# Seven small reorderings in a four-layer kernel whose order is written out by hand: weights and norms, MLP rows, image loads of a spectral layer, products of an attention, and idle matmuls

## The chip, the cores and the metric

The kernel runs on one core of one Trainium2 chip, in fp32. The time is what the device takes for one execution, in microseconds (us). TensorE is called PE, VectorE DVE, ScalarE ACT, GpSimd POOL; SP is the queue that issues most of the transfers (DMA). PE and its weight load (PEld) are shown apart.

## The reference, cut to what matters

The input x has the shape (4, 56, 56, 128): batch, rows, columns, channels. Four layers are added to it in turn, each after a group norm `_gn` over 32 groups.

```python
x = x + L0(_gn(x))      # windows 7x7 shifted by 3, 4 heads; then global attention; then an MLP
x = x + L1(_gn(x))      # edge layer
x = x + L2(_gn(x))      # spectral attention and two spectral MLP layers
x = x + L3(_gn(x))      # convolution over rows, sums over rows and columns

# L0, the second half, on xf = (B, 3136, 128)
xf = xf + _mha(_layernorm(xf, g1, be1), ...)
h = gelu(_layernorm(xf, g2, be2) @ w1 + b1)         # 128 -> 512
xf = xf + (h @ w2 + b2)                             # 512 -> 128

# L1
edge = relu(proj_i[:, :, :, None, :] + proj_j[:, :, None, :, :] + be)
node = relu(concat([x, edge.sum(axis=3)]) @ Wn.T + bn)

# L2: each of the (batch, row) images is 56 columns x 128 channels, normed; 32 heads
k, q, v = spectral convolutions of the normed image   # rfft2, 16x16 modes kept at both ends, irfft2
attn = softmax(q k^T / sqrt(d))                       # over the 56 rows
projd = spectral convolution of attn @ v
attention = inorm(projd + x)
m = gelu(inorm(spec(inorm(attention))) + skip); m = inorm(spec(m)) + skip
out = inorm(m) + attention

# L3
y = conv(x, W, kernel 3 over rows) + b
out = relu((y.sum(columns) + y.sum(rows) - y) / sqrt(H + W - 2) + x)
```

## The kernel before, in words

The function `build` runs the stages one after the other. Every engine executes its instructions in the order in which the program writes them, so that the Python order of the calls, and of `next(...)` on generators that emit a few instructions each, is the schedule. Transfers on SP are issued in order too: a request that waits for an engine holds those behind it.

*Input norms* (`input_norms`, 0 to 50 us). The four images of 128 x 3136 are loaded and normed as they land (`norm_steps`), and the lengths of the largest query and key vectors are bounded (`products`, `longest`). The generator `weights` puts pieces between: `score_bounds`, `attention_bias` (b_p, L906 to L923) and `edge_weights`. `fill(n)` emits n idle matmuls `z_p<-c_ones` of 128x384, each in two passes, to keep PE at work. The last one is `fill(4)`, ahead of the first real matmul, L375.

*Four batches* (50 to 2587 us). Each runs `fast_windows` (the shifted windows), `fast_layer` (global attention and MLP) and `edge_layer`. The attention works on seven query blocks of 448; `values(room)` issues the products with the values as chunks get ready, and `remainder(j)` one odd chunk of block j. The MLP takes eight row groups: `hidden(wi)` makes four matmul pairs into banks (L779) and GELUs on ACT (L780), `result(wi)` four more into the bank `pm[:, 4]` (L800), which DVE adds to the row (L802) and POOL (for the last one DVE) adds to the image (L813, L815). L770 is DVE's norm of a row group, which the `hidden` of that group reads.

*Spectra* (`spectra`, 2587 to 2668 us). For each of the four images `first_transform` does the transform along the columns in four pieces of 14 rows (`s_pr<-t_images,s_x`, L1655), and `sample_spectra` the rest (L1671, L1683, L1693). The images 0 to 2 come from the scratch `xad` in two halves each, in two buffers `s_x2`; image 3 is still in the tile `x1`. `normed_images` norms image 3 in steps (`go_on(n)` takes n of them): statistics, then four pieces of 128x784 normed on DVE by `apply_norm`, and its transfer to `xat`. `all_score_weights` and `value_weights` compute the weights of the attention, mostly on POOL (L1750 to L1796); their inputs come by SP.

*Attention weights* (`attention_weights`, 2668 to 2801 us). For two pairs of images (bp) and sixteen channels c, the spectrum times the weights `q_g` is built as `q_u`, one half on DVE (L1864, n = 0) and one on POOL (L1862, n = 1), and PE multiplies it with the spectrum into `q_acc` (L1877, 16 matmuls each). The list `seq` gives the order; `make` runs four items ahead of `product`. After sixteen channels `collect` copies `q_acc` to y, and `softmax` turns y (L1911, L1919) into weights; `skips` prepares the skip terms.

*Attend* (`attend`, 2801 to 3123 us). DVE (`u_ud`, L2018) and POOL (`u_up`, L2020) build scaled images, and PE mixes them with the weights `AT` into `u_po` (L2023).

*Outputs* (`outputs`, 3123 to 3463 us). Projection, norms, spectral MLP and the convolution (L2683) of all batches are operations of a class `Plan`, issued in an order that is written out as a list of numbers (`OUTPUT_ORDER`). PE's small matmuls on `o_sq` (L2339) and `o_r` (L2366) make sums and norms there; L2272 and L2255 are transforms.

Of the kernel before, what the change touches and what calls it, by code (L numbers as in the profile page):

```python
# [19 lines left out]
P = 128  # L20
# [603 lines left out]
def fast_layer(k, w, xw, xf, x1, st, beside, mr, shift):  # L624
# [9 lines left out]
    with ExitStack() as es:  # L634
# [158 lines left out]
        def result(wi):  # L793
            ts, hT = parts[wi], made.pop(wi)
            po = pm[:, 4, :N]
# [21 lines left out]
        with tc.manual_schedule(engines={mybir.EngineType.PE, mybir.EngineType.Activation, mybir.EngineType.DVE}):  # L817
# [31 lines left out]
            while t < 96 * NBLK:  # L849
                scores(0)  # L850
                scores(1)
                values(ROOM[turn % 4] + (len(ready) > 3))
# [3 lines left out]
                if special < NBLK and t >= 96 * special + 7 and (not special or hasattr(blocks[special - 1], "raw")):  # L856
                    j = special
                    special += 1
                    remainder(j)
# [32 lines left out]
            for wi in range(3, 8):  # L892
                if wi < 7:
                    hidden(wi + 1)
                result(wi)
# [65 lines left out]
def input_norms(k, x, pool, wk, psum, weights):  # L961
# [49 lines left out]
    fill(2)  # L1011
    next(steps[3])
    next(steps[3])
    products(2)
    longest(2)
    next(work)
    next(work)
    products(3)
    next(work)
# [6 lines left out]
    for _ in range(2):  # L1026
        next(work)
# [524 lines left out]
def normed_images(k, w, st, b, wk, bank, xp, xad, xat):  # L1552
# [49 lines left out]
    nc.vector.tensor_scalar_mul(mean, mean, mr[:, 1:2])  # L1602
    yield
# [16 lines left out]
    def normed():  # L1620
        for t in range(0, HH, 14):
            apply_norm(k, x[:, t:t + 14, :], x[:, t:t + 14, :], mr)
            if t < 42:
                yield
# [17 lines left out]
def first_transform(k, st, b, pools, x, to):  # L1642
# [7 lines left out]
    xf = x.rearrange("p t h -> p (t h)")  # L1650
# [48 lines left out]
def spectra(k, w, st, xat, images):  # L1699
# [7 lines left out]
    with ExitStack() as es:  # L1707
# [7 lines left out]
        first = [first_transform(k, st, b, (wk, psum), st.x1 if b == B - 1 else images(b), zs) for b in range(B)]  # L1715
# [10 lines left out]
        fill(3)  # L1726
        go_on(28)
        next(first[0])
        next(first[0])
        go_on(1)  # L1730
        fill(4)
        next(first[0])
        go_on(1)
        next(first[0])
        go_on(2)
        for b in range(B):
            for n, _ in enumerate(sample_spectra(k, st, b, (wk, psum), zs.pop(b))):
                go_on(2)
# [72 lines left out]
def attention_weights(k, I, w, st):  # L1811
# [9 lines left out]
    with ExitStack() as es:  # L1821
# [21 lines left out]
        for bp in range(2):  # L1843
            for c in range(16):
                seq += [(bp, c, 0, None), (bp, c, 1, None)]
                if c in (8, 10, 12, 14):
                    seq.insert(len(seq) - 1, (bp, None, c // 2 % 2, c // 12))

# [76 lines left out]
        ahead = 4  # L1925
        for item in seq[:ahead]:
            make(*item)
        for n, item in enumerate(seq):
# [12 lines left out]
            if n >= 3 and between and next(between[0], 0) == 0:  # L1941
# [7 lines left out]
def attend(k, I, w, st, dd, xat, xm, softmax, beside, psum):  # L1949
# [4 lines left out]
    with ExitStack() as es:  # L1954
# [50 lines left out]
        late = []  # L2005
        prepare(0)
        for turn, (g, n, bp) in enumerate(turns):
# [5 lines left out]
            for i in range(2):  # L2013
                for h0, m, e in (shares if turn else first)[left < 16]:
# [6 lines left out]
                    for q in range(m):  # L2021
# [4 lines left out]
                        left -= 1  # L2026
                    for step in steps.get((turn, left), ()):
# [149 lines left out]

class Plan:
# [4 lines left out]
    def __init__(self, **buffers):  # L2183
        self.ops, self.buffers = [], buffers
# [8 lines left out]
    def issue(self, order):  # L2193
# [7 lines left out]
        for n in order:  # L2201
            op = self.ops[n]
            assert all(a.end for a in op.after)
            for b, key in op.takes:
                taken[b].append(key)
                old = len(taken[b]) - 1 - self.buffers[b]
                assert old < 0 or not users[b, taken[b][old]]
            op.run()
            op.end = True
            for g in op.gives:  # L2210
                users[g] -= 1

# [556 lines left out]
def outputs(k, w, st, ys, x2d, xm, out, psum):  # L2769

    tc = k.tc
    with ExitStack() as es:
# [3 lines left out]

        def bank():
            return psum.tile([P, 512], F32, tag="b", name="o_b")

        def banks():  # L2780
            taken[0] += 1
            tag, bufs = ("x", 1) if taken[0] % 3 == 0 else ("px", 2)
            return psum.tile([P, 2, 512], F32, tag=tag, name="o_d", bufs=bufs)
# [20 lines left out]
        for b, op in ((1, wholes[3].spread[0]), (2, wholes[3].factors)):  # L2804
            for p in wholes[b].convolve:
                p.after.append(op)
        plan.issue([int(n) for n in OUTPUT_ORDER.split()])
# [29 lines left out]
def build(k, packs, I, out):  # L2837
# [3 lines left out]
    with ExitStack() as es:  # L2841
# [9 lines left out]
        x1 = x1w[:, :HH, :]  # L2851
        dd = dp.tile([3, 4, 2, 16, NB], F32, name="dd")
# [5 lines left out]
        with tc.tile_pool(name="w01", bufs=1) as wp, tc.tile_pool(name="io", bufs=1) as io:  # L2858
            xw = io.tile([P, TOK], F32, name="xw")
            with ExitStack() as pre:  # L2860
# [18 lines left out]
                def weights(ps):  # L2879
                    yield from score_bounds(k, w0, bounds, wk, ps)  # L2880
                    added = attention_bias(k, w0, wp)
                    edge_weights(k, w1, wp)
                    yield
                    added()
                    yield
# [4 lines left out]
                small_scores = scores_are_small(k, bounds, wp, wk)  # L2890

            def first_layers(front, x, to, loaded=False):
# [4 lines left out]
                front(k, w0, xw, xf, x1, st)  # L2897
                edge_layer(k, w1, x1, st)
# [14 lines left out]
            with small.Else():  # L2913
# [4 lines left out]
                with tc.tile_pool(name="n_x", bufs=2) as xs, tc.tile_pool(name="n_ps", bufs=2, space=PSUM) as psum:  # L2918
                    for b in range(B - 1):
                        xp = xs.tile([P, HH, HH], F32, name="n_x")  # L2920
                        nc.sync.dma_start(xp, x2d[b])
                        for _ in normed_images(k, w2, st, b, io, lambda: psum.tile([P, 512], F32, name="n_ps"), xp,
                                               xad, xat):
                            pass

        x2s = ExitStack()
        x2p = x2s.enter_context(tc.tile_pool(name="x2", bufs=2, side="right"))

        def images(b):
            if b not in loaded:  # L2930
                xp = loaded[b] = x2p.tile([P, HH + 1, HH], F32, name="s_x2")
                for o in (slice(0, 29), slice(29, HH)):
                    nc.sync.dma_start(xp[:, o, :], xad[b, :, o, :])
                nc.gpsimd.memset(xp[:, HH, :], 0.0)
            return loaded[b]

        loaded = {}
        for b in range(2):
            images(b)
        nc.sync.dma_start(x2d[B - 1], x1)  # L2940
# [52 lines left out]
```

## Time and profile before

| | us |
|---|---|
| median of three runs | 3463.82 (3462.63 to 3465.51) |
| the profiled execution | 3464.84 |
| its span in the profile | 3463.1 |

The profile's span is from the first to the last instruction of the profiled execution; that execution's own time is 1.0 us over the median. Its granted clock, the TensorE clock that the throttle allowed, has a mean of 0.993 of full speed.

| stage | window, us | length | PE busy |
|---|---|---|---|
| input norms | 0 to 50.14 | 50.14 | 29.27 |
| four batches | 50.14 to 2587.2 | 2537.06 | 2459.28 |
| spectra | 2587.2 to 2668 | 80.80 | 76.49 |
| attention weights | 2668 to 2801.4 | 133.40 | 123.08 |
| attend | 2801.4 to 3122.7 | 321.30 | 316.39 |
| outputs | 3122.7 to 3463.1 | 340.40 | 314.51 |

A row of a wait names the engine, the tile and the line that waited, and behind the arrow the engine and line that came last. A row of the timeline has the start, the length, the operation with its output and inputs, the count of passes, and in brackets the idle time before it and its releaser. A matmul of fp32 takes two passes in these counts, so that one idle matmul is x2.

### The profile page before, as it was taken

What the parts mean: (1) busy time and instruction counts of PE and PEld (TensorE: products, weight loads), DVE (VectorE), ACT (ScalarE), POOL (GpSimd) and SP (SyncE); (2) the same over time, 40 slices, a digit from 0 to 9 for tenths busy, and PEclk for the clock granted to TensorE, in tenths of its full rate; (3) what the DMA queues carried; (4) which work ended last, traced back from release to release, by engine and by line L of the source; (5) the groups of instructions that cost most, each with busy time, mean ns of one, the idle gap of its engine ahead of it and who ended that gap; (6) DMA issues with size and microseconds to landing.
All of it is one profiled execution on the core that took longest, in us unless ns stands there. A gap on an engine that the chain in (4) does not pass through costs nothing. (4 is left out here: it accounts for less than half of the span.)

```text
span 3463.1 us, 64456 instructions
## 1 busy us (share of the span) xinstructions
PE 3319.0 (96%) x27800; PEld 1425.6 (41%) x27800; DVE 2657.9 (77%) x2555; ACT 2131.1 (62%) x2253; POOL 1285.9 (37%) x796
## 2 busy tenths in 40 slices
PE   7999999999999999999999999999999999999998
PEld 4433333353333435333343443333337433336664
DVE  6588867867888696788859858887794778895776
ACT  4688876668888575788857668887653012215442
POOL 1000007800000491000019400000775778884786
PEclk9999999999999999999999999999999999999999
DMA  2143420024434000444310033442014037743101
GB/s 106 43 94 89 97 54 19 20 53 93 92 91 86 19 1 20 106 103 91 91 42 1 20 81 90 93 97 54 1 40 118 1 87 187 190 115 94 57 20 56
DMA packets 98012, 243.41 MB, mean 70 GB/s; under 512 B 64457, under 2 KB 69833, under 8 KB 92713
## 3 DMA queue, kind: packets, MB, share of 16 engines
q0 software_dynamic: 16128, 102.77, 14.8%
q1 hardware_dynamic: 74872, 123.61, 12.2%
q10 hardware_dynamic: 6720, 12.85, 1.3%
q8 instruction: 220, 3.60, 0.4%
q14 instruction: 72, 0.58, 0.1%
HBM read 79.43 MB, written 31.33 MB: 32 GB/s over the span
## 5 line engine op out<-in xcount | busy, mean ns | idle before, releaser
L830 ACT ACTIVATE f_ring<-f_pm 128x1792 f32<-128x1792 f32 (+1 forms) x764 | 1093.8, 1482 | 226.4 <-PE f_pm L827 179.6
L682 DVE TENSOR_TENSOR f_acc<-f_acc,f_ring 128x1792 f32<-128x1792 f32 x468 | 947.5, 2025 | 190.2 <-ACT f_ring L830 160.0
L827 PE MATMUL f_pm<-f_qT,f_kT 32*128 32x448 f32 x5376 | 722.6, 571 | 9.9 <-ACT f_p L716 4.1
L672 POOL DMA_DIRECT2D f_far<-f_ring x112 | 96.5, 862 | 1328.2 <-ACT f_ring L830 1033.4
L693 PE MATMUL f_pm<-f_ring,f_va 128*32 128x448 f32 (+1 forms) x6304 | 589.4, 490 | 0.0
L1269 POOL TENSOR_TENSOR e_tp<-e_a,e_c 128x1792 f32<-128x1792 f32 (+2 forms) x172 | 480.4, 2831 | 36.7 <-issue 36.7
L1267 DVE TENSOR_TENSOR e_td<-e_a,e_pc 128x1792 f32<-128x1792 f32 (+2 forms) x292 | 478.3, 1703 | 8.8 <-ACT e_c L1255 8.8
L827 PEld LDWEIGHTS f_pm<-f_qT,f_kT 32*128 32x128 f32 x5376 | 260.2, 183 | 411.5 <-ACT f_ring L830 300.3
L693 PEld LDWEIGHTS f_pm<-f_ring,f_va 128*32 128x32 f32 x6304 | 163.8, 109 | 410.1 <-issue 397.8
L1271 ACT ACTIVATE e_tp<-e_tp 128x1792 f32<-128x1792 f32 (+2 forms) x172 | 253.3, 1495 | 98.0 <-POOL e_tp L1269 98.0
L2018 DVE TENSOR_TENSOR u_ud<-u_px,u_d 112x1792 f32<-112x1792 f32 x144 | 263.4, 1863 | 39.7 <-PE u_po L2023 35.1
L2020 POOL TENSOR_TENSOR u_up<-xh,u_d 112x1792 f32<-112x1792 f32 (+1 forms) x72 | 240.9, 3373 | 55.0 <-PE u_po L2023 40.7
L1338 PE MATMUL e_acc<-e_td,t_edge 128*32 128x448 f32 x1952 | 231.6, 542 | 6.6 <-DVE e_td L1267 6.4
L2023 PE MATMUL u_po<-u_ud,AT 112*64 112x448 f32 x1056 | 213.9, 544 | 1.9 <-DVE u_ud L2018 1.9
L1338 PE MATMUL e_acc<-e_tp,t_edge 128*32 128x448 f32 x1184 | 147.9, 543 | 23.7 <-ACT e_tp L1271 23.7
L2023 PEld LDWEIGHTS u_po<-u_ud,AT 112*64 112x64 f32 x1056 | 74.3, 138 | 128.9 <-issue 112.8
L1338 PEld LDWEIGHTS e_acc<-e_td,t_edge 128*32 128x32 f32 x1952 | 61.6, 110 | 142.6 <-issue 93.7
L737 DVE RECIPROCAL f_den<-f_den 128x448 f32<-128x448 f32 x28 | 82.6, 2951 | 44.9 <-ACT f_den L734 44.9
L1862 POOL TENSOR_TENSOR q_u<-iS,q_g 128x1792 f32<-128x1792 f32 x32 | 102.8, 3235 | 22.8 <-PE q_acc L1877 22.8
L813 POOL TENSOR_TENSOR x<-xf,xw 128x343 f32<-128x343 f32 x28 | 25.5, 911 | 224.7 <-DVE xf L802 224.7
L1877 PE MATMUL q_acc<-q_u,S 64*64 64x448 f32 x1024 | 104.4, 552 | 4.4 <-DVE q_u L1864 3.3
L2121 ACT COPY x_ev<-x_po 56x896 f32<-56x896 f32 x32 | 28.8, 900 | 126.9 <-DMA x_xs<-xat 51.1
(525 smaller groups left out, 4579.1 us busy)
## 6 DMA issues: line engine op xcount, KB each, us to landing
f_far<-f_ring POOLq DMA_DIRECT2D x112, 896.0 KB, 6.4
u_d<-dd SPq DMA_DIRECT2D x46, 784.0 KB
f_far<-f_ring SPq DMA_DIRECT2D x28, 896.0 KB
xw<-in_x SPq DMA_DIRECT2D x4, 1568.0 KB
x2d<-x SPq DMA_DIRECT2D x4, 1568.0 KB
xat<-x SPq DMA_DIRECT2D x4, 1568.0 KB
x_xs<-xat ACTq DMA_DIRECT2D x32, 196.0 KB
xm<-x_ev ACTq DMA_DIRECT2D x64, 98.0 KB
```

The costliest lines, as they stand in the source:

```text
L682: nc.vector.tensor_add(e.acc, e.acc, slots(j, c))
L693: nc.tensor.matmul(e.po[heads[h], part], va[o, c, heads[h]], p, start=(c == 0), stop=(c == 23 and part.stop == NB))
L827: nc.tensor.matmul(ss[:, i, :NB], kT[heads[h], c * P:(c + 1) * P], qT[heads[h], blk(j)], start=True, stop=True)
L830: nc.scalar.activation(ring[:, slot:slot + m, :], ss[:, :m, :NB], AF.Exp, scale=scale)
L1267: nc.vector.tensor_tensor(t, am, cm, ALU.max)
L1269: nc.gpsimd.tensor_sub(t, am, cm)
L1271: nc.scalar.activation(tf, tf, AF.Relu)
L1338: nc.tensor.matmul(acc[quarters[r0 + r], :NB], w.S[:, 0, :], t[:, r].rearrange("p l n -> p (l n)"), start=(g == 0), stop=(g == len(turns) ...
L1877: nc.tensor.matmul(acc[bp][i][halves[hb % 2], hb // 2, :NB], x[o], u[o, 8 * hb:8 * hb + 8, :].rearrange("p h t -> p (h t)"), start=first, ...
L2018: nc.vector.tensor_mul(u, bc(px[:, :, :NB], 2, m), dm)
L2020: nc.gpsimd.tensor_mul(u, bc(x, 2, m), dm)
L2023: nc.tensor.matmul(po[64 * b2:64 * b2 + 64, :NB], st.AT[:, 8 * i + h0 + q, 2 * bp + b2, :], u[:, b2, q, :], start=(left == 16), stop=(left ...
```

## The change

1. In `input_norms`, `attention_bias` is issued between the norms of images 2 and 3 and `longest(2)` directly behind `products(2)`; `fill(2)` becomes `fill(1)`, and `weights` yields one time less behind the last matmul `i_pt`.
2. In `fast_layer`, `remainder(0)` is called between two calls of `values`.
3. In the MLP, `result(3)` is issued ahead of `hidden(4)`, and `result(5)` and `result(7)` write a second bank, `pm[:, 5]`.
4. In the spectra, image 0 is loaded to the tile `xw` of the batches (`first_image`), which is kept; image 2 goes to the same tile, image 1 to the only other. The loads of all weights (`bulk`) and the transfer of `x1` to `x2d` are issued behind the request for image 2. `fill(3)` and `go_on(28)` at the start are gone. The norm of image 3 is spread over the first samples, and its four pieces run on ACT.
5. In `attention_weights`, the item of POOL stands one channel later than that of DVE in the first pass; `q_idle` gets four idle matmuls at the start; the steps of `between` are spread in the second pass.
6. In `attend`, four idle matmuls stand at the start and two behind the first matmul group.
7. In the outputs, idle matmuls are emitted at eight places of the order: in the bank that an operation opens (`FILL_OWN`) or in a spare bank (`FILL_SPARE`).

```diff
@@ result / the MLP's order
-            po = pm[:, 4, :N]
+            po = pm[:, 4 + (wi > 3 and wi % 2), :N]
...
-            for wi in range(3, 8):
+            result(3)
+            hidden(4)
+            for wi in range(4, 8):
                 if wi < 7:
                     hidden(wi + 1)
                 result(wi)
@@ values
-                values(ROOM[turn % 4] + (len(ready) > 3))
+                room = ROOM[turn % 4] + (len(ready) > 3)
+                if not special and t >= 7:
+                    values(2)
+                    remainder(0)
+                    room -= 2
+                values(room)
...
-                    remainder(j)
+                    if j:
+                        remainder(j)
@@ input_norms
     longest(1)
-    fill(2)
-    next(steps[3])
+    fill(1)
     next(steps[3])
     products(2)
     longest(2)
+    next(steps[3])
     next(work)
     next(work)
     products(3)
-    next(work)
     longest(3)
...
-    for _ in range(2):
-        next(work)
+    next(work)
@@ weights
-                    yield from score_bounds(k, w0, bounds, wk, ps)
+                    steps = score_bounds(k, w0, bounds, wk, ps)
+                    next(steps)
                     added = attention_bias(k, w0, wp)
+                    yield
+                    next(steps)
+                    added()
                     edge_weights(k, w1, wp)
                     yield
-                    added()
-                    yield
+                    yield from steps
@@ normed_images (image 3)
+                nc.scalar.activation(x[:, t:t + 14, :], x[:, t:t + 14, :], AF.Identity, bias=t1, scale=mr[:, 1:2])
@@ spectra
-        fill(3)
-        go_on(28)
-        next(first[0])
-        next(first[0])
-        go_on(1)
-        fill(4)
-        next(first[0])
-        go_on(1)
-        next(first[0])
-        go_on(2)
+        for n in range(4):
+            next(first[0])
+            if n == 2:
+                fill(4)
+        images(2)
+        bulk()
...
-                go_on(2)
+                go_on(4 if b == 0 and n < 7 else 2 if b and n > 8 else 1)
@@ build
+            def first_image():
+                nc.sync.dma_start(xi[:, :HH, :], xad[0])
+                nc.gpsimd.memset(xi[:, HH, :], 0.0)
...
+                    def bulk():
+                        all_score_weights(k, I, w2, sp, wk, st)
+                        value_weights(k, I, w2, wk, dd)
+                        nc.sync.dma_start(x2d[B - 1], x1)
+                        load_weights(k, l3p, I, "w3_", w2)
+                        load_weights(k, l3p, I, "w2_", w2, only=CONV_WEIGHTS)
@@ attention_weights
-                seq += [(bp, c, 0, None), (bp, c, 1, None)]
+                seq.append((bp, c, 0, None))
+                if bp or c:
+                    seq.append((bp, c - (not bp), 1, None))
...
+        idle = psum.tile([P, 512], F32, tag="t", name="q_idle", bufs=1)
+        for _ in range(4):
+            nc.tensor.matmul(idle[:, :3 * P], k.ident, bc(k.ones, 1, 3), start=True, stop=True)
...
-            if n >= 3 and between and next(between[0], 0) == 0:
+            if n >= 3 and between and (item[0] == 0 or n % 4 == 2 and n > 38) and next(between[0], 0) == 0:
@@ attend
+        fill(4)
         prepare(0)
...
+                    if not turn and left == 15:
+                        fill(2)
@@ outputs
+FILL_OWN = {42: 1, 82: 1, 330: 1, 743: 2, 748: 2}
+FILL_SPARE = {30: 1, 160: 1, 273: 2}
...
+            if n in FILL_SPARE:
+                self.idle = FILL_SPARE[n]
...
+                self.spare()
+            self.idle = FILL_OWN.get(n, 0)
```

## The prediction

> **What bounds the kernel now.** I read the busy totals first, then a table of busy time by stage, then what TensorE (PE) waits for, then PE's timeline around each wait, with its granted clock.
>
> ```profile
> PE 3319.0 (96%) x27800; PEld 1425.6 (41%) x27800; DVE 2657.9 (77%) x2555; ACT 2131.1 (62%) x2253; POOL 1285.9 (37%) x796
> ```
>
> PE runs for 3319.0 of 3463.1 us. A change that takes no matmul away can win only idle time of PE (144 us in all) and time in which PE runs at half clock. Where is that? By stage (columns: window, length, busy time of PE, PEld, DVE, ACT, POOL, granted clock, DMA share, GB/s):
>
> ```profile
> 50.14:2587.20 2537.06, 2459.28 (x21063) 967.98 (x21064) 1989.04 (x1726) 1861.45 (x1844) 647.23 (x459) 1.00 0.26 59
> 2587.20:2668.00 80.80, 76.49 (x1224) 65.25 (x1222) 37.23 (x114) 31.19 (x69) 36.06 (x57) 0.96 0.47 142
> 2668.00:2801.40 133.40, 123.08 (x1376) 57.18 (x1376) 96.23 (x57) 8.57 (x13) 102.94 (x33) 0.96 0.07 16
> ```
>
> These are the four batches, the spectra and the attention weights. The batches have full clock and small waits that come four times; the two others have idle PE and a clock of 0.96. The waits of PE that the change aims at (total, times, longest):
>
> ```profile
> PE q_pt L1919 <- DVE y L1911: 5.9, 1, 5.9
> PE f_pm L779 <- DVE f_oT L770: 3.4, 4, 0.9
> PE q_acc L1877 <- DVE q_u L1864: 3.3, 1, 3.3
> PE f_pm L800 <- DVE xf L802: 3.2, 4, 0.8
> PE u_po L2023 <- POOL u_up L2020: 2.4, 1, 2.4
> PE u_po L2023 <- DVE u_ud L2018: 1.9, 1, 1.9
> ```
>
> The timeline of PE (start, length, operation, idle before) shows what follows a wait:
>
> ```profile
> 44.71 5.28 PE L991 MATMUL z_p<-c_ones 128*1 128x384 f32 x8
> ...
> 2595.11 2.85 PE L1721 MATMUL s_pt<-c_ones,t_shared 128*128 128x384 f32 x8
> ...
> 2747.02 1.10 PE L1919 MATMUL q_pt<-t_shared,y 128*112 128x128 f32 x4 [5.88 <-DVE y L1911]
> 2748.05 2.97 PE L1877 MATMUL q_acc<-q_u,S 64*64 64x448 f32 x16
> 2750.95 0.65 PE L1919 MATMUL q_pt<-t_shared,y 128*112 128x128 f32 x4
> 2751.53 1.75 PE L1877 MATMUL q_acc<-q_u,S 64*64 64x448 f32 x16
> ```
>
> Sixteen q_acc matmuls take 2.97 us after the wait and 1.75 later: half clock costs 1.2 us there, and 0.45 on the four before. The first two rows price a filler (a matmul for nothing, in two passes): 5.28/4 = 1.32 us cold, 2.85/4 = 0.71 warm.
>
> **The change part by part.** The sum is made against the profiled execution (3464.84 us, 1.0 over the median 3463.82).
>
> *Input norms.* Sixteen b_p passes (1.95 us, 41.73 to 43.68) and their DVE and POOL steps move ahead of the last image's statistics; one filler goes. The chain of the last image is pushed back: its L942 by about 1.9 us (31.96 to 33.9), its squares by some 3 us less what the earlier maximum over image 2 gives back, so i_pt stays near 41.4. Behind i_pt nothing is left but the four fillers, which end at 49.99 now, cold, and hold the first L375 to 50.14. They would end near 47 or earlier; then ACT's w_xg and the norm before it set the start, about 48 to 49. I take -1.5; ends -2.5 and +1 (if the longer chain to i_pt wins).
>
> *First remainder between values.* In the instruction order of PE and ACT nothing moves: where the new call stands, only one group is ready. 0.
>
> *MLP.* Result(3) goes ahead of hidden(4), which now waits 0.85 us for DVE's L770 (3.4/4); result(3) is 2.8 us of PE that needs nothing new. Result(7) gets another bank, so it no longer waits 0.81 for L802 to free the old one. I leave 0.05 of it, since DVE's tail behind it is as long. The two hidden blocks now back to back ask ACT for eight GELUs of about 0.6 us (L780) against 0.66 us of PE each (2.80 in four), so ACT keeps up. 4 x 1.6 = -6.4; ends -7 and -3.
>
> *Spectra.* Image 0 is loaded during the last edge layer (2540 to 2590 has a DMA share of 0.05), so seven fillers become four, the 0.94 and 0.80 us waits go, and bulk weight loads are issued on SP after images 1 and 2. PE's work from 2588.75 is then four first transforms in quarters (4 x 1.75 = 7.0 us each, from two at 3.46), 2.85 of fillers and four samples of 9.7, plus 1.2 of norm: 28 + 2.85 + 38.8 + 1.2 = 70.8; with 1.7 of small waits (0.4 to 0.5 each, as at 2602.08) 72.5, against 79.2 now. Some of the difference is the half-clock stretch 2610.6 to 2617.3, where 40 s_pr take 2.04 us and 16 s_px 3.33 against 1.83 later. I take -6.7. A new wait: image 2 goes into image 0's tile, so its request waits on SP until PE has read image 0, at about 2598. Behind it on SP stand V, P, x2d and the w3/w2 weights, which nobody reads for tens of us. Its 1.6 MB take about 4 us at the 413 GB/s that the DMA row reaches here, up to 12 shared with the rest, so it lands by 2610; PE needs it near 2618. Moved instructions: SP issues qk, V, P, x2d and the w3/w2 weights behind the images; POOL's value weights, which now start at 2605.6, start about 10 us earlier; they run some 37 us and end near 2634, ahead of the first q_u at 2668. The four norm pieces of batch 3 go from DVE to ACT: the nearest row, an ACTIVATE of 128x784, takes 0.857 us (L2430), so 3.4 us on an engine busy for 31.19 of 80.80. They stand in ACT's order ahead of copies that free PE's banks, so one can hold PE up to 0.86 us. Ends -3 (four such holds, or image 1 late) and -8.
>
> *Attention weights.* In the first pass POOL's product now stands one channel later than DVE's, and the softmax and skip steps are spread. The 5.88 us wait goes to about 0.9 (the collect before it still needs its last product: DVE's y copy at L1896 costs 1.1 now and stays): -5.0. The dip behind it goes: -1.65. Four fillers run into the 3.3 us wait for the first q_u (2.85 warm: inside it), and spare the dip at 2672 to 2675, 1.5 us. Together -8.2; ends -3 and -9.
>
> *Attend.* Fillers 4 and 2 lie in waits of 2.4 and 1.9 us. After them DVE's u_ud (1863 ns each) sets the pace until PE has caught up at 2816, so warmth buys nothing: 0; ends -1 and +1.
>
> *Outputs.* Eleven fillers (11 x 0.71 = 7.8 us) at eight places; the gaps there are 0.67, 0.72, 1.00, 0.66, 0.85, 1.34, 1.23 and 1.32, together 7.8. They are spent inside waits and cost nothing while warm; cold they overrun by 14.5 - 7.8 = 6.7. The gain is the last convolution at full clock:
>
> ```profile
> 3410.72 0.85 PE L2339 MATMUL o_b<-o_sq,c_ones_px 128*32 128x392 f32 x4 [1.23 <-ACT o_sq L2391]
> 3411.86 0.85 PE L2339 MATMUL o_b<-o_sq,c_ones_px 128*32 128x392 f32 x4 [0.29 <-ACT o_sq L2391]
> 3414.04 1.03 PE L2366 MATMUL o_b<-o_r,slot 128*128 128x7 f32 x8 [1.32 <-DVE o_r L2355]
> 3414.92 15.47 PE L2683 MATMUL o_d<-o_x,o_wr 128*128 128x448 f32 x36
> ```
>
> The same 36 matmuls took 13.80 at 3258: 1.7 us. The gap at 3399 costs 1.4 likewise (16 o_d in 2.99 against 1.60). -2.0 of these 3.1; ends -3.5 and +2.
>
> [...] The profile has PE busy 8.03 of 10 us at clock 1.00 and then half clock:
>
> ```profile
> 2600.00:2610.00 10.00, 8.03 (x130) 6.06 (x127) 5.29 (x21) 5.51 (x13) 2.46 (x9) 1.00 0.76 259
> 2610.00:2620.00 10.00, 10.00 (x144) 9.63 (x145) 4.96 (x6) 1.11 (x2) 9.80 (x17) 0.66 0.48 191
> ```
>
> The longest gap in the first row is 1.09 us. [...]
>
> Sum: -1.5 - 6.4 - 6.7 - 8.2 + 0 - 2.0 = -24.8; 3464.8 - 24.8 = 3440.0 profiled, 3439.0 as a median.
>
> **The rivals.**
>
> *A: attention becomes bound by POOL.* L1862 takes 3192 ns, PE's two products of a channel 3.2 to 3.5. For: at 2738 two took 7.72, 3.86 each, while DVE was busy 9.86 of 10. Against: the median of 32 is 3192. If the sixteen of one pass take 3.86, (3.86 - 3.19) x 16 = 10.7, less slack of some 2: +9, so 3448.
>
> *B: only idle time goes.* The dips come at other places (-1.65, -1.5, -2.0 not won) and the spectra give 3.5 less because ACT's pieces and image 2 hold PE: 3439 + 8.6, about 3447. [...] against, that dips follow PE's gaps here.
>
> *C, slower: fillers in the path.* They stand in PE's order whether a wait is there or not. If the reordering ahead has moved or closed the waits and PE is cold, the 21 in attention, attend and outputs cost 21 x 1.32 = 27.7. Idle time that goes without any clock gain is 1.5 + 6.4 + 3 + 5 = 15.9; new dips, three of 1.5, add 4.5. 27.7 + 4.5 - 15.9 = +16, at 3480; half of it, 3471, if the first waits stay. It decides beyond 22.8 us of uncovered filler and dips (15.9 + 6.9). Against: the waits at 2668 and 2801 start stages, where nothing else can fill them.
>
> *D: it does more.* Both dips in the outputs and the full spectra: 3431. That one part does nothing (the remainder) is counted already.
>
> **How the numbers follow.** 0.2%, 6.9 us, is about what a measurement of this kernel can tell from no change. The sum 0.62 (3434 to 3445), A 0.12, B 0.18, C 0.03, D 0.05. The time is 3439. The range, 3431 to 3452, takes in A and B with the ends of the parts. Faster than 3456.9: nearly all of the sum, B and D, and most of A: 0.94. C lies above 3470.7: 0.03; 0.03 is left between.
>
> **What would show it.** The batches about 1.6 us shorter each, with L770 and L802 gone from PE's waits; the spectra near 74 us with clock 0.98 or more; attention near 125 with no wait over 1.5 at L1919; q_u on POOL still 3192 ns; 36 o_d in 13.8 us near the end. It is wrong if fillers run at 1.3 us each with no wait around them, if POOL's products come late all through the first pass, or if the spectra show PE waiting for s_x or for ACT.

## The result, and the profile after

The changed kernel takes 3450.56 us (median of five, 3445.68 to 3464.64), the kernel before beside it 3465.28; the ratio is 0.9964 (0.9954 to 0.9975), some 12 to 15 us faster. The forecast was 25 us, to 3439: right in direction, almost twice too large. The time lies within the range of 3431 to 3452, near its slow end.

The profiled execution happens to be the slowest of the five, 3464.64 us with a span of 3462.8. So I show a second profile of the same code beside it (label e1_after_again, 3451.27 us, span 3449.5). Busy time of the first:

```profile
PE 3337.5 (96%) x27834; PEld 1441.2 (42%) x27834; DVE 2659.6 (77%) x2552; ACT 2134.9 (62%) x2257; POOL 1284.9 (37%) x795
```

PE is busy for 18.5 us longer than before with only 34 more passes: these are the same matmuls at a lower clock (granted 0.991 against 0.993). By stage (batches, spectra, attention weights, attend, outputs), first profile:

```profile
47.59:2584.14 2536.55, 2462.76 (x21064) 971.64 (x21064) 1994.70 (x1727) 1862.07 (x1845) 648.96 (x465) 1.00 0.26 61
2584.14:2664.81 80.67, 74.99 (x1225) 63.45 (x1225) 36.77 (x112) 36.36 (x76) 36.88 (x55) 0.98 0.48 126
2664.81:2791.48 126.67, 122.36 (x1386) 57.52 (x1385) 97.61 (x58) 7.87 (x11) 105.94 (x34) 1.00 0.04 9
2791.48:3108.12 316.64, 315.49 (x1773) 117.73 (x1773) 274.21 (x170) 67.68 (x102) 262.30 (x90) 1.00 0.63 156
3108.12:3462.80 354.68, 336.02 (x2256) 219.31 (x2254) 226.72 (x398) 144.41 (x207) 222.63 (x136) 0.94 0.19 55
```

and the last of these rows in the second profile of the same code:

```profile
3108.07:3449.50 341.43, 323.41 (x2256) 209.57 (x2254) 226.52 (x398) 144.15 (x207) 222.53 (x136) 0.98 0.20 57
```

The stages ahead of the outputs repeat within 0.5 us; the outputs differ by 13 us for the same instructions. Where the gain stands, measured by the start of a marker operation against the first profile of before:

| up to | after | second profile | forecast of the step |
|---|---|---|---|
| first windows running (w_po) | -1.19 | -1.28 | -1.5 |
| last edge layer (e_pa of batch 3) | -3.68 | -3.40 | -6.4 more |
| attention's first q_acc | -6.47 | -6.50 | -6.7 more |
| first matmul of the outputs | -14.58 | -14.63 | -8.2 more |
| last matmul | -0.23 | -13.56 | -2.0 more |

The batches give 2.1 to 2.5 instead of 6.4, the spectra 2.8 to 3.1 instead of 6.7, attention and attend 8.1 as forecast, the outputs nothing, or a loss of 14. One profile of before is a weak base for such steps. Against its second profile (e10_before_again below) the input norms give nothing (+0.3 to +0.4), the batches the same 2.1 to 2.5, the spectra 1.4 to 1.7, attention and attend 7.6 to 7.7. Only the batches and the attention stand clear of this.

What answers to the waits shown of before is this:

```profile
PE w_mm L375 <- ACT w_qd L223: 10.5, 5, 2.7
PE s_pr L1666 <- issue: 3.6, 2, 2.2
PE x_po L2026 <- DVE y L1908: 2.2, 1, 2.2
PE q_acc L1889 <- DVE y L1908: 1.1, 1, 1.1
PE q_acc L1889 <- DVE q_u L1876: 0.9, 1, 0.9
```

The 5.9 at the softmax and the MLP's 3.4 are gone, and the first q_u's 3.3 is down to 0.9. In their place the first row has grown (6.0 before). A row with the releaser "issue" is new, that is a wait which no semaphore explains. The x_po row is the idle matmuls of attend, which wait where u_po had waited 2.4.

### The profile page after: what moved, and what is told of

Read it like the earlier page. It is cut to its first block, busy times and chain, and to the rows that moved or that the text cites. A ratio compares the mean times of both kernels' runs of the same rounds, so it can differ in the third digit from the quotient of the medians.

```text
span 3462.8 us, 64536 instructions
## 1 busy us (share of the span) xinstructions
PE 3337.5 (96%) x27834; PEld 1441.2 (42%) x27834; DVE 2659.6 (77%) x2552; ACT 2134.9 (62%) x2257; POOL 1284.9 (37%) x795
## 5 line engine op out<-in xcount | busy, mean ns | idle before, releaser
L2145 ACT COPY x_ev<-x_po 56x896 f32<-56x896 f32 x32 | 28.8, 900 | 126.7 <-DMA x_xs<-xat 57.8
```

## The experiments

**The same kernel again (e1_after_again).**

> The changed kernel once more, for more executions and a second profile. Theory H (the half-clock stretch of 34.1 us at 3303, [...]belongs to that one execution): the profile's stages up to 3108 repeat within 1 us (windows start 47.6, attention's first q_acc 2664.8, outputs start 3108), most executions lie at 3445 to 3452, and a long half-clock stretch is absent or sits elsewhere. Rival (it belongs to the changed order): the same stretch comes again at 3303 and the time is 3464.

3451.22 us (3444.88 to 3453.86), ratio 0.995 (0.9937 to 0.9963). The stages repeat; the 34 us stretch at half clock does not. It began in a gap that before has too, 1.19 us ahead of the same operation (first pair after, second pair before):

```profile
3303.65 0.97 PE L2376 MATMUL o_b<-o_t,c_ones 112*32 112x224 f32 x8 [1.19 <-ACT o_t L2365]
3304.56 3.33 PE L2345 MATMUL o_d<-o_z,t_images 56*112 56x448 f32 x8
```

```profile
3318.47 0.59 PE L2339 MATMUL o_b<-o_t,c_ones 112*32 112x224 f32 x8 [1.19 <-ACT o_t L2328]
3318.99 1.76 PE L2308 MATMUL o_d<-o_z,t_images 56*112 56x448 f32 x8
```

In the one execution PE went on at 3.33 us for eight, in the other at 1.76. In the second profile of the changed code a shorter stretch came earlier, with PE busy all the time before it:

```profile
3275.00:3280.00 5.00, 5.00 (x45) 4.25 (x44) 2.84 (x7) 4.96 (x7) 4.92 (x4) 0.97 0.02 4
3280.00:3285.00 5.00, 5.00 (x17) 2.70 (x17) 5.00 (x4) 1.27 (x3) 5.00 (x3) 0.50 0.80 160
```

In the clock records of before and after, the half-clock stretches (granted 0.50) behind 60 us and ahead of the end last 3.41, 6.83 or, at 3303.33 in after, 34.13 us. So the place and length of these stretches belong to the execution and not only to the code. A stage's time from one profile holds a share of that chance.

The records say more about this chance. The stretches of one profile start whole multiples of 3.413 us apart: in after, from 1316.77 to 1955.07, 2593.36, 3303.33 and 3398.90, it is 187, 187, 208 and 28 times; in before, from 2610.63 to 2672.07, 2743.75, 2805.19, 3399.11 and 3416.18, it is 18, 21, 18, 174 and 5 times. In the 3.413 us ahead of each of these eleven PE was busy for 0.79 to 2.34 us. But of the other pieces of 3.413 us at full clock in the two profiles, from 60 us to the last matmul and counted from the starts of the stretches, 45 held less than 2.4 us of PE's work too, and no half clock followed them. So a gap of PE does not settle whether half clock comes: the one of 1.19 us had it in one execution and not in the other. Three stretches near 3280 (e1, e3, e11) and one at 3160 (e5) came with no gap of PE ahead of them; for these the cause is open.

**The norm on ACT (e2_norm_on_act).**

```diff
-            if g < 2:
+            if g < 3:
                 nc.scalar.activation(out, x, AF.Identity, bias=shift, scale=mr[:, 1:2])
```

> The changed kernel, with the third row group's norm (w_xg, L193) at each start of the windows on ACT instead of DVE. Theory M (the MLP's 1.7 us a batch is given back because DVE's L193, 3.61 us where 0.48 is usual, is held while POOL clears the windows' tiles, and DVE's w_qd behind it holds PE 2.74 us): PE's wait at L375 falls to about 1 us in each batch, the four batches shorten by 4 to 6 us, the kernel stands at 3441 to 3446. Rival (PE waits for ACT or for something else at that place as well): the wait stays at 2 us or more under another name, and the time is within 1.5 us of the changed kernel.

3443.01 us (3441.71 to 3445.93), ratio 0.9935 (0.9923 to 0.9948). No wait of that row is longer than 1.1 us any more:

```profile
PE w_mm L375 <- ACT w_qd L223: 6.6, 8, 1.1
```

and the last edge layer begins 9.34 us earlier than before, instead of 3.68. The MLPs are the same in both, 1.7 us shorter each. What took their gain begins with one instruction of DVE at the start of the next windows. DVE's rows in before, then in after:

```profile
680.15 1.14 DVE L193 TENSOR_SCALAR w_xg<-xw,mr 128x392 f32<-128x392 f32 x1
684.55 2.08 DVE L193 TENSOR_SCALAR w_xg<-xw,mr 128x392 f32<-128x392 f32 x1
```

```profile
677.20 3.61 DVE L193 TENSOR_SCALAR w_xg<-xw,mr 128x392 f32<-128x392 f32 x1
683.35 0.51 DVE L193 TENSOR_SCALAR w_xg<-xw,mr 128x392 f32<-128x392 f32 x1
```

The median of L193 is 0.479 us. Beside the 3.61 POOL clears the tiles of the windows:

```profile
676.72 1.41 POOL L340 MEMSET w_qd<- 128x1568 f32 x1
...
678.16 0.98 POOL L343 MEMSET w_vd<- 128x1056 f32 x1
...
679.13 1.41 POOL L340 MEMSET w_qd<- 128x1568 f32 x1
680.47 0.40 POOL L345 MEMSET w_vd<- 64x16 f32 x2
```

DVE gets through near 680.8, behind several of these. Its next instruction, w_qd, is what ACT's w_qd and then PE wait for: 2.74 us at 683.28, where before had 0.99. By itself this costs 0.7 us from the first w_mm to the first w_po (13.75 against 13.03). At two of the three starts in each of the two profiles half clock came with the wait (in after at 1316.77 for 6.8 us and at 1955.07 for 3.4), and there the loss was 1.5 to 2.9.

**The same norm with two inputs (e11_norm_two_inputs).**

```diff
+            elif g == 2:
+                nc.vector.scalar_tensor_tensor(out.rearrange("p (n o) -> p n o", o=1), x.rearrange("p (n o) -> p n o", o=1),
+                                               mr[:, 1:2], bc(shift, 1, N), ALU.mult, ALU.add)
             else:
                 apply_norm(k, out, x, mr)
```

> The changed kernel, the third row group's norm still on DVE at the same place, but as an operation with two inputs (scalar_tensor_tensor, x times scale plus the shift spread over the row) instead of the tensor_scalar of L193. Theory M [...]: it takes 0.5 to 0.8 us at all four starts, PE's wait at L375 is about 1 us, the time that of e2_norm_on_act, 3443. Rival (DVE is held by [...]a late semaphore or the order): it still takes 1.1 to 3.6 us and the time stays at 3450.

3445.88 us (3445.53 to 3447.31), ratio 0.9945 (0.9932 to 0.9959). On the same engine, at the same place, beside the same clearing:

```profile
L370 DVE SCALAR_TENSOR_TENSOR w_xg<-xw,mr,shift x4: 616/617/627, 46.6 to 1943.7; 128x392 f32<-128x392 f32 x4
```

0.62 us at all four starts, and the wait at L375 is 6.6 in all, as with ACT. So what took 3.61 us beside the clearing is this form of DVE's instruction, and the cause was neither its place nor a semaphore. That POOL is what holds it is my reading of the overlap: no run took the clearing away, and why the form matters is not shown. The last edge layer starts 8.94 us earlier than before, within 0.4 of the version with ACT; the other 2.5 us between the two kernels arise in their spectra and outputs.

**The MLP alone (e6_mlp_alone).** On the kernel before:

```diff
-            po = pm[:, 4, :N]
+            po = pm[:, 4 + (wi > 3 and wi % 2), :N]
...
-            for wi in range(3, 8):
+            result(3)
+            hidden(4)
+            for wi in range(4, 8):
```

> The kernel before with the MLP's part of the change alone (result(3) ahead of hidden(4), results 5 and 7 in the second bank). As predicted: 1.6 us a batch, 6.4 in all. Theory M (what it wins is given back where POOL's clearing holds DVE at the next windows): each MLP 1.7 us shorter; if the collision depends on the exact timing alone, it may or may not come here: L193 at 3.61 us and 2 to 3 us in all, or L193 at 1.14 and 2.08 as before and the full 6.4 to 6.9.

3455.37 us (3453.09 to 3460.07), ratio 0.9975 (0.9967 to 0.9983), 8.7 us by the ratio. Each MLP is 1.7 us shorter. The collision comes once:

```profile
677.27 3.61 DVE L193 TENSOR_SCALAR w_xg<-xw,mr 128x392 f32<-128x392 f32 x1
...
1312.22 1.14 DVE L193 TENSOR_SCALAR w_xg<-xw,mr 128x392 f32<-128x392 f32 x1
1316.62 2.08 DVE L193 TENSOR_SCALAR w_xg<-xw,mr 128x392 f32<-128x392 f32 x1
```

Batch 1 loses 1.5 us at that place, batches 2 and 3 nothing. That makes 5.4 us up to the last edge layer; the rest of the 8.7 is not the MLP's, as its profile has the unchanged spectra at 76.2 us instead of 80.2. The same code meets both cases in one execution. It does so in e7_attention_order_alone below too, whose batches are those of before (3.61 us at 679.72). DVE's row starts 484 to 486 ns behind POOL's first large clearing in both cases, so what decides is not in the trace. In the profiles of the changed order with L193 on DVE (after, e1, e3, e4) it is 3.61 at all three starts. The forecast's MLP step was right as a step.

**The weights' loads by ACT (e4_weights_by_act).**

```diff
-    load_weights(k, wk, I, "w2_", w, ("qk", "qkr", "qk4"))
+    load_weights(k, wk, I, "w2_", w, ("qk", "qkr", "qk4"), queue=nc.scalar)
```

(the same for V, Vrev and P, and for the transfer to x2d)

> The changed kernel, with the loads of the attention's weights (qk, qkr, qk4, V, Vrev, P) and the x2d transfer issued by ACT behind image 0's transform, instead of by SP at 2583 to 2594. Theory S [...]: the gap and the cold filler go, the spectra shorten by 3 to 4 us. Rival (the gap comes from elsewhere, image 1's transfer or the program's own code): it stays, and the spectra change by less than 1 us.

Theory S put the gap of 2.24 us in image 0's third quarter down to the transfers that SP issues there. The gap went, and with it the cold filler behind it (4.54 us, 2.85 here); the time did not follow: 3460.59 us (3455.09 to 3474.23), ratio 0.9987 (0.9978 to 0.9996). PE at image 0 in after, and then here:

```profile
2585.47 3.54 PE L1666 MATMUL s_pr<-t_images,xw 128*64 128x33 f32 x115 [1.33 <-issue]
2591.26 1.76 PE L1666 MATMUL s_pr<-t_images,xw 128*64 128x33 f32 x53 [2.24 <-issue]
2592.95 4.54 PE L1733 MATMUL s_pt<-c_ones,t_shared 128*128 128x384 f32 x8
```

```profile
2582.84 5.24 PE L1666 MATMUL s_pr<-t_images,xw 128*64 128x33 f32 x168 [1.37 <-issue]
2588.01 2.85 PE L1733 MATMUL s_pt<-c_ones,t_shared 128*128 128x384 f32 x8
```

From the first s_pr to the first s_ps it is 10.51 us, against 14.51. But the later weights put more of POOL's small operations beside DVE's statistics:

```profile
2612.80 11.92 DVE L1595 TENSOR_TENSOR s_d<-s_rows 128x56 f32<-128x56 f32 x1
```

```profile
2632.54 0.67 PE L1614 MATMUL s_pt<-s_mean,c_ones_c 128*128 128x56 f32 x2 [11.77 <-DVE s_mean L1608]
```

An operation of 0.25 us (in before) took 11.92, while POOL ran some 18 operations back to back, and PE stood for 11.77. Half clock came with it, from 2622.66 for 23.9 us. It looks like the collision of the windows. But no run tests that, and in after the same operation took 0.25 (at 2617.87) beside a POOL operation of 1.40 (from 2617.13), so what made the difference is open.

**Fillers ahead of the third quarter (e5_fill_before_third).**

```diff
-            if n == 2:
+            if n == 1:
                 fill(4)
```

(with the norm on ACT)

> The kernel with the third group's norm on ACT, and the spectra's four fillers ahead of image 0's third quarter instead of behind it. Theory S (PE runs out of instructions 115 s_pr passes into image 0, [...]the gap was 1.7 to 2.2 us in four profiles and absent where the weights came later): [...]the gap shrinks to under 0.5 us, no cold filler (2.85, not 4.1 to 5.0), first s_pr to first q_acc 76 us instead of 79: about 3440. Rival (PE waits there for data or for a bank): the gap stays at 1.7 or more and the time is as before, 3443.

```profile
2580.05 3.46 PE L1666 MATMUL s_pr<-t_images,xw 128*64 128x33 f32 x112 [1.25 <-issue]
2583.44 1.24 PE L1733 MATMUL s_pt<-c_ones,t_shared 128*128 128x384 f32 x3
2585.83 1.88 PE L1733 MATMUL s_pt<-c_ones,t_shared 128*128 128x384 f32 x5 [1.16 <-issue]
2587.64 3.46 PE L1666 MATMUL s_pr<-t_images,xw 128*64 128x33 f32 x112
```

The gap keeps its place in the instruction count, 112 and 3 passes here and 115 there, whatever the instructions are: these fillers wait for no new data. So the gap is tied to a place in PE's order and not to data; that PE has no instructions there is my reading of it. The gap fell to 1.16 us, not to under 0.5 as expected. First s_pr to first s_ps is 11.79 against 14.06 with the norm alone. But a further gap of this kind later in the same spectra (1.28 us at 2637.49) and a half-clock stretch of 3.4 us behind it took the 2.3 back (79.07 to the first q_acc, against 78.88), and the time is 3445.61 us (3442.58 to 3446.45), ratio 0.9941 (0.9928 to 0.9955): no faster than 3443.01.

The profile's list of queues has one of the kind "instruction", q8, with 220 packets of 16 KB in after. A packet of it begins 3.4 us after the first s_pr in after, 2.8 in the second profile, and 1.1 where the weights came later. In all 14 profiles, every gap of PE over 1 us with the releaser "issue" behind 60 us, 23 of them and 1.0 to 3.3 us long, ends 2.2 to 3.1 us after the start of such a packet, those ahead of the first s_pr too (in after 3.14 us for the gap of 1.33, and 2.37 for that of 2.24). That is a tie in time; that PE waits for the packet, and what sets the packet's time, is not shown. The transfers take about all of the DMA engines' time at this place (a share of 0.99 at 2586 to 2588 in after), but so they do in before (1.02 at 2592 to 2594), where a packet begins 0.7 us after the first s_pr and no such gap follows.

**Only part of the loads moved (e12_values_by_act).** On e8 below, with qk as in the change:

```diff
-    load_weights(k, wk, I, "w2_", w, ("V", "Vrev", "P"))
+    load_weights(k, wk, I, "w2_", w, ("V", "Vrev", "P"), queue=nc.scalar)
...
-                        nc.sync.dma_start(x2d[B - 1], x1)
+                        nc.scalar.dma_start(x2d[B - 1], x1)
```

> As e8_two_more_fills (3442.9), with the loads of V, Vrev and P and the transfer to x2d issued by ACT behind image 0's transform; qk stays where it was, so that POOL starts its work as early as before. Theory S: with 0.9 MB less in flight at 2584 to 2589 the gap at 115 passes shrinks below 1 us; POOL's chain ends no later and doesn't meet DVE's statistics as it did in e4_weights_by_act; 0.5 to 1.5 us faster than e8. Rival: POOL's chain moves into DVE's statistics again and PE waits several us at L1614: slower than e8.

3442.93 us (3441.75 to 3443.6), ratio 0.9936 (0.9923 to 0.995), the same as e8. The gap stayed at 1.48 us, so moving V and P is not what ended it in e4; that moving the loads of qk did is what remains of e4 against this; it was not tried alone, so it is not shown.

**All but the spectra's part (e9_all_but_spectra).** On e2, point 4 of the change taken back (spectra, normed_images, first_transform and build's buffers and loads); of its diff:

```diff
-        for n in range(4):
-            next(first[0])
-            if n == 2:
-                fill(4)
-        images(2)
-        bulk()
+        fill(3)
+        go_on(28)
...
-                go_on(4 if b == 0 and n < 7 else 2 if b and n > 8 else 1)
+                go_on(2)
```

> The changed kernel with the norm on ACT (as e2_norm_on_act, 3443.0), but with the spectra's part of the change undone: image 0 loaded at the stage's start, seven fillers, the weights' loads where they were, image 3 normed on DVE. As predicted (the part is worth 6.7): slower by 6 to 7, near 3450. Theory Z (unchanged spectra take 76.2 and 76.5 us in two profiles without a half-clock stretch, changed ones 76.5 to 77.6; the 80.2 of the first profile was that stretch): the same within 2, with spectra of about 76.5 or, where a half-clock stretch falls into them, about 80.

3448.83 us (3448.09 to 3454.82), ratio 0.9966 (0.9952 to 0.9979). Against e2 the part is worth some 6 us by the medians (11 by the ratios), but not where I had put it. From the last e_idle to the last s_px it is 78.1 us here and 76.5 with the part, 1.6, and unchanged spectra took 76.2 and 76.5 in e6 and e7; so a gain inside the spectra is not shown. The rest comes behind it. Attention takes 132.1 us to the first u_po, against 126.7:

```profile
2665.20 1.55 PE L1898 MATMUL q_pg<-R 64*64 64x56 f32 x90
2670.01 1.33 PE L1898 MATMUL q_pg<-R 64*64 64x56 f32 x43 [3.27 <-issue]
```

Here SP issues the u_d loads at 2659.5, and PE stands for 3.27 us in the middle of q_pg; in after they are issued at 2630.9, among the spectra. A half-clock stretch of 3.4 us follows the gap. That these loads make the gap is argued, not tested: in before, e10 and e6 SP issues them at the same place, 0.8 us behind the first q_acc, and there is no gap. A packet of q8 begins 1.3 to 1.6 us behind the first q_acc in those three, and 8.5 here. My theory Z, that the part is worth nothing, falls for the kernel.

**The attention's order alone (e7_attention_order_alone).** On the kernel before:

```diff
-                seq += [(bp, c, 0, None), (bp, c, 1, None)]
+                seq.append((bp, c, 0, None))
+                if bp or c:
+                    seq.append((bp, c - (not bp), 1, None))
...
+            if not bp:
+                seq.append((bp, c, 1, None))
...
-            if n >= 3 and between and next(between[0], 0) == 0:
+            if n >= 3 and between and (item[0] == 0 or n % 4 == 2 and n > 38) and next(between[0], 0) == 0:
```

> The kernel before with the attention's new order of products and steps alone, without its four idle matmuls. As predicted: the 5.88 us wait at L1919 becomes 0.9 (5.0) and the dip behind it goes (1.65), 6.6 in all; the dip at 2672 stays. If POOL becomes the bound in the first pass: 0 to 3, with L1862 at 3.8 us.

3460.8 us (3455.7 to 3468.95), ratio 0.9992 (0.9984 to 1.0001). From the first q_acc to the outputs it is 446.94 us. Three profiles with the old order have 451.42, 450.95 (before) and 449.41 (e6): 2.5 to 4.5, with a gap at q_pg of 2.23 us that these lack. Less that gap it would be 4.7 to 6.7, and the forecast was 6.6. POOL's product keeps its 3.19 us, so rival A is out. The gap comes in the two profiles that have the new order with the late u_d loads (e7, e9) and in none with the early ones, so the order seems to need these to keep its gain.

**The outputs' fillers (e3_no_output_fill, e8_two_more_fills).** e3, on the changed kernel, and e8, on e5:

```diff
-FILL_OWN = {42: 1, 82: 1, 330: 1, 743: 2, 748: 2}
-FILL_SPARE = {30: 1, 160: 1, 273: 2}
+FILL_OWN = {}
+FILL_SPARE = {}
```

```diff
-FILL_OWN = {42: 1, 82: 1, 330: 1, 743: 2, 748: 2}
+FILL_OWN = {42: 1, 82: 1, 330: 1, 374: 1, 464: 2, 743: 2, 748: 2}
```

> The changed kernel without the eleven idle matmuls of the outputs. As predicted: slower by 2 (the dip at 3416 comes back, 1.7 us, and nothing else). If the fillers hold nothing by themselves: within 1 us. If they lie in the path: faster by up to 4.

> As e5 (fillers ahead of the third quarter), with three more idle matmuls in the outputs: two in the 1.19 us gap ahead of L2376 at 3302, one at 3276 ahead of L2403, where another profile fell to half clock with no gap at all. Theory C ([...]its place differs from one execution to the next): long stretches in 3270 to 3340 become rarer, the executions lie closer together, the median 0 to 2 us below e5. Rival (the fillers are too short to matter, or the stretch starts elsewhere): the median is 0.5 to 1 us above e5 and the spread the same.

Without fillers: 3453.29 us (3447.41 to 3461.72), ratio 0.9962 (0.9949 to 0.9975), 2 to 3 us above the changed kernel's medians, with intervals that overlap. What the fillers hold is seen at the last convolution, in after and then without them:

```profile
3415.20 13.78 PE L2720 MATMUL o_d<-o_x,o_wr 128*128 128x448 f32 x36
```

```profile
3410.49 16.76 PE L2720 MATMUL o_d<-o_x,o_wr 128*128 128x448 f32 x36
```

It was 15.47 in before. In all nine profiles with these fillers it is 13.78; of the five without, four have 15.47 to 16.76 and one (e7) 13.78. The stage as a whole shows no gain: from its first to its last matmul it takes 327.4 to 330.2 us in the four profiles with unchanged outputs, and 327.7 to 330.7 in those with the fillers, but 343.1 in after and 339.5 without them in e3. With three more fillers: 3442.86 us (3441.31 to 3443.74), ratio 0.9936 (0.9923 to 0.995), 2.8 below e5 and with a smaller spread. Its profile has full clock from 3255 to 3340, but so has that of e5. Five executions do not prove that the stretches are rarer; the median agrees with theory C, and that is all.

**Before again (e10_before_again).**

> The kernel before once more, for a second profile. If its half-clock stretches belong to the code: at 2610, 2672, 2744, 2805, 3399 and 3416 again, spectra 80.2 us, attention weights to outputs 451.4. If their places differ from one execution to the next: one or two of them missing or one more elsewhere, and spectra of 76 to 77 or 80.

3462.82 us. The spectra from the last e_idle to the last s_px take 78.77, against 80.17 in the first profile, 76.20 in e6 and 76.54 in e7, four times the same code. The half-clock stretches near 2744, 2805, 3399 and 3416 recur, the first of them longer (10.2 us instead of 6.8), the second shorter (3.4 instead of 6.8); that at 2672 is missing, that in the spectra is 3.4 us instead of 6.8 and lies at 2600, and one at 3168 is new.

## Why the prediction was wrong

Two steps failed above all. The sum took the MLP's gain as the batches' gain, and 5.1 of 6.9 us were lost at the start of the next windows. And it took the spectra of one profile, with a half-clock stretch in them, as what the code costs, and put waits of PE that no semaphore explains at nothing.

*Input norms*: -1.5 forecast, -1.2 to -1.3 measured against the first profile of before. L375 starts 2.6 us earlier, and half of that is gone again by the first w_po; with the norm on ACT 1.65 are left, so L193 (1.77 and 2.63 us there) is a part of it and not all. The agreement is partly luck: the first w_po starts at 60.8 to 62.4 us in four profiles with the old input norms (before, e10, e6, e7) and at 60.0 to 61.2 in four with the new (after, e1, e3, e4).

*First remainder*: 0 and 0.

*MLP*: -6.4 forecast, -6.9 measured at the MLPs (e6 and both profiles of after), and 5.1 given back at the starts of batches 1 to 3 (some 2.2 by the wait alone, some 2.9 by the half clock that came with it). The step that failed is the one I didn't write: what is next on the path. The stage table showed small waits that come four times, and w_qd L223 with 6.0 us stood fourth among PE's waits; I didn't ask why DVE's L193 behind it took 1.14 and 2.08 us where 0.48 is usual.

*Spectra*: -6.7 forecast, -2.8 to -3.1 to the first q_acc against the first profile of before. From the last edge layer to the first q_acc unchanged spectra take 215.5 to 219.4 us (before, e10, e6, e7, e9), changed ones 215.9 to 217.8 (after, e1, e2, e3, e11): a gain of the stage itself is not shown. Three terms were mis-sized. The wait ahead of the first s_pr stays (0.94 counted as won; 1.03 to 1.33 measured), now with the releaser "issue". The gap in image 0, with the same releaser, costs 1.7 to 2.2, and up to 1.7 more where the fillers behind it are cold (4.54 against 2.85). And the half-clock stretch of 6.8 us that I read as the stage's is 3.4 or absent in other executions of before. The loads did not go behind both images, as I wrote: in SP's queue qk and V stand ahead of image 2. What I missed on the other side, some 5 us, is what the part saves in attention (e9); it is contained in attention's figure below.

*Attention and attend*: -8.2 and 0 forecast, -5.8 and -2.3 measured, -8.1 together; against the second profile of before -5.4 and -2.3, against e6 -3.8 and -2.3. So the agreement of the sums is partly luck. The wait went to 1.1, not 0.9. The warm start of attend is worth the 2.3 that I gave to nobody: I had DVE set its pace until 2816, but PE's first u_po of u_ud fell from 3.25 us to 1.72 and the gain stayed (before, then after):

```profile
2806.60 3.25 PE L2023 MATMUL u_po<-u_ud,AT 112*64 112x448 f32 x8 [1.86 <-DVE u_ud L2018]
```

```profile
2793.87 1.72 PE L2045 MATMUL u_po<-u_ud,AT 112*64 112x448 f32 x8
```

*Outputs*: -2.0 forecast. The last convolution gained its 1.7 in both profiles; the dip at 3399 stays in the first and is absent in the second. Against it stand stretches at half clock in other places: the second profile loses 1.1 in this stage, the first 14.4.

*The fillers' ground*: I took the dips of before to follow PE's gaps of about 1 us, and used that as if a filler in a gap settled the matter. The stretch at 3279 (e1) came with no gap in PE's rows at all, and the gap of 1.19 us was followed by half clock in after and by full clock in before. That dips come at other places, which I had left to rival B, was worth more than the step: the first profile lost 14.4 us in this stage, against 2.0 forecast as a gain.

Of the rivals B came nearest, at 3447 and with its reason: dips at other places and 3.5 us less from the spectra. Its holder of PE was neither ACT nor image 2, and it counted the batches' 6.4 in full, so its nearness is partly luck.

The best versions tried are e2, e8 and e12, all at 3443 us: the change, with the norm of the third group on ACT.

## What to carry to other kernels

When a stage gets shorter, look at the first instructions of the next one, above all at any whose duration varies from row to row: here 0.48 us grew to 3.61 beside another engine's clearing, and another form of the instruction (0.62) or another engine ended that. Moving a load also moved PE's gaps without a semaphore (2.24 us in after, gone in e4; 3.27 in e9) and what else was on POOL and DVE at that time; e4 and e5 won at their place and lost it behind. And take stage times with half-clock stretches from more than one execution, before they are counted as a gain.

## What the runs showed of the hardware

- In after a TENSOR_SCALAR of DVE (L193) took 3.61 us at 677.20 beside POOL's clearing (1.41, 0.98, 1.41 and 0.40 us), where the line's median is 0.48. With two inputs the same norm took 0.62 in e11 beside the same clearing. That POOL holds it is a reading of the overlap. (The 11.92 for 0.25 of e4 looks alike; its cause is not shown.)
- PE stood 1.33 and 2.24 us in after and 3.27 in e9 with no semaphore to explain it. In e5 the gap, 1.16 us there, came at 115 passes as in after, though other instructions stood at that place. The 23 such gaps of the 14 profiles end 2.2 to 3.1 us behind the start of a packet of the queue "instruction"; that PE waits for it is not shown.
- Half clock (granted 0.50) came in stretches of 3.41, 6.83 and 34.13 us in before and after, with starts whole multiples of 3.413 us apart within a profile. In the 3.413 us ahead of each PE was busy for 0.79 to 2.34 us, but 45 other pieces of that length with less than 2.4 had no half clock behind them, and in e1 a stretch came behind 5.00 busy us of 5.00. In the stretch of 34.13 us PE was busy for 33.81.
